# Writing out the order of three engines in the prologue of a two-layer graph network kernel

## The chip, the cores and the metric

The kernel runs on one core of a Trainium2 chip. The metric is the device time of one execution in microseconds (us). A core has five engines, each with its own instruction queue that runs in order: TensorE (PE, matrix products into PSUM), VectorE (DVE), ScalarE (ACT), GpSimd (POOL) and SyncE (SP, which here only issues DMAs). ScalarE and GpSimd issue DMAs from their queues too. An engine waits for another one through semaphores. "PEld" is the loading of weights into TensorE, a row of its own in the profile.

## The reference, cut to what matters

There are 6250 nodes with 128 features and 206250 edges, sorted by destination. Each edge has a type from 0 to 8.

```python
h = jnp.maximum(_layernorm(x), 0.0)
deg = segment_sum(ones, src);  norm = clip(deg, 1.0) ** -0.5
x = x + relu(segment_sum((h * norm)[src], dst)) @ W0.T + b0
h = jnp.maximum(_layernorm(x), 0.0)
msg = h[src] @ W_msg.T + b_msg + edge_embed[edge_type]
m = segment_sum(msg, dst)
x = x + gru_cell(m, h, W_ih, W_hh, b_ih, b_hh)
```

## The kernel before

The edge list is turned into a dense adjacency matrix of edge counts, 49 by 49 blocks of 128 by 128 (`NB` = 49), and each layer multiplies it from the left with a table of node features. The kernel has four stages.

**Prologue, edges** (lines 367 to 526). The lists `dst`, `src` and `etype` come in as tiles of 128 x 1616 integers (`dst_i`, `src_i`, `typ_i`), edge number j at partition j mod 128. Each is reduced to a small number per edge: `dst_f`, `low_b` (source mod 128), `code_b` (source div 128), `typ_b`. TensorE turns them by products with the identity (line 496), in four steps of `k0` with up to four column blocks each, and they are copied from PSUM to `turned` as 16-bit integers: fields 1 and 2 (code and type) by VectorE (line 506), fields 0 and 3 by ScalarE (line 508). SP writes them to a list in DRAM, `flat` (lines 516 and 521). Meanwhile a search finds where the edges of each window of 250 nodes begin: `heads` (every 128th destination) against `starts` gives `base_ps`, a product on TensorE (line 407); from it the addresses `base_i`, with which GpSimd fetches `span` (line 416); `search` compares it (line 446), `search_sums` adds up (line 454), and `last_of_search` turns the result into `row_i`, the row of `flat` at which each window starts (lines 468 to 484). The 49 blocks of x are loaded by SP in eight DMAs (lines 381 to 386); `stats` takes the layernorm statistics of a block (line 464).

**Prologue, windows** (lines 529 to 777). 25 windows are handled in seven groups of four (the last of one). `fetch` gathers the rows of `flat` from `row_i` (line 627, one indirect DMA per window on GpSimd), marks the edges that lie `inside` the window (641), masks the `fields` (648), turns them on TensorE (657), and ScalarE copies the types to `typ` and the code and low parts to `code_t` and `lo_t` (667, 670). `count` makes a mask per edge type, five on VectorE (`m_dve`, 682) and four on ScalarE (`m_act`, 685), sums them per node on TensorE (686) and copies the sums to `counts` (689). For each of seven chunks of seven blocks (`CB` = 7, `NCH` = 7), `degrees` sums the counts (696) and makes `scale` (704, square root on ScalarE 708), `rows_of` makes the reciprocal, `shift_`, and the scaled rows f (718 to 735), and `terms_of` splits them into the tables `tab1` (739 to 747): three bf16 terms in chunk 0 (`NARROW` = 1), two fp32r terms in the others. One pass of the loop at line 749 calls `degrees(i - 3)`, `fetch` of group i, `count` of group i - 1, then `rows_of` and `terms_of` of chunk i - 3. GpSimd also splits the small matrix `rest` in three (759, 761).

**First layer** (lines 803 to 931). The columns of the matrix are made in chunks (`FRONT`: one of 128 columns, then 24 of 256). `hots` makes a pair of one-hot tiles for 64 columns on VectorE (336), `build` multiplies them on TensorE (823) and ScalarE copies the counts to `adj` (832). While chunk c is built, the sums of chunk c - 1 run (`sums`, line 791): TOTAL = 105 products a chunk, spread over eight rounds. Those with `tab1[1]` and up need the matrix as fp32r (`cast`, 896, by ScalarE and VectorE in turn). SP writes `adj` to DRAM (929).

**Second layer** (lines 937 to 1085). It reads the matrix back, sums in the same way, and does the GRU.

What sets the order: inside `tc.manual_schedule(engines=...)` the instructions of the engines named keep the order of the program text. Before, VectorE alone is named in the prologue, and a scheduler places those of TensorE and ScalarE; in the first layer all three are named. A tile of a pool is reused when it is free; `reuse_waits="tile"` makes the wait for that one per tile.

Of the kernel before, what the change touches and what calls it, by code (L numbers as in the profile page):

```python
# [10 lines left out]
F32 = mybir.dt.float32  # L11
# [20 lines left out]
CB = 7  # L32
# [226 lines left out]
def by_matrix(  # L259
# [107 lines left out]
    with tc.tile_pool(name="pro", bufs=1) as pro, tc.manual_schedule(engines={mybir.EngineType.DVE}):  # L367
# [13 lines left out]
        for c in range(NCH):  # L381
            lo, hi = c * CB, min((c + 1) * CB, full)
            nc.sync.dma_start(
                out=xs[:, lo:hi, :], in_=x[lo * P : hi * P, :].rearrange("(b p) f -> p b f", p=P)
            )
        nc.sync.dma_start(out=xs[:tail, full, :], in_=x[full * P : N, :])
# [19 lines left out]
        for j in range(GT):  # L406
            nc.tensor.matmul(base_ps, less[:, j, :], one_b[:NG, :], start=(j == 0), stop=(j == GT - 1))
        base = pro.tile([P, 1], F32, name="base")
# [14 lines left out]


        dst_f = raw.tile([P, NT], F32, name="dst_f")
        nc.scalar.copy(dst_f, dst_i)
        low_i = raw.tile([P, NT], I32, name="low_i")
        nc.vector.tensor_scalar(low_i, src_i, P - 1, None, op0=ALU.bitwise_and)
        low_b = raw.tile([P, NT], BF16, name="low_b")
        nc.scalar.copy(low_b, low_i)  # L430
        nc.vector.tensor_scalar(src_i, src_i, 7, None, op0=ALU.logical_shift_right)
        code_b = raw.tile([P, NT], BF16, name="code_b")
        nc.vector.tensor_copy(code_b, src_i)
        typ_b = raw.tile([P, NT], BF16, name="typ_b")
        nc.vector.tensor_scalar(typ_b, typ_i, 0.0, float(TYPES - 1), op0=ALU.max, op1=ALU.min)
# [52 lines left out]
        for k0 in range(0, NT // P + 1, 4):  # L488
            k1 = min(k0 + 4, NT // P + 1)
            n = min(P, NT - k0 * P)  # L490
            for i, given in enumerate((dst_f, code_b, typ_b, low_b)):
# [17 lines left out]
            if k0 == 0:  # L509
                stats(8)  # L510
            if k0 == 4:
                search()
            if k0 == 8:
                search_sums()
# [22 lines left out]
        wnd = look.enter_context(tc.tile_pool(name="wnd", bufs=2))  # L537
        pps = look.enter_context(tc.tile_pool(name="turn_ps", bufs=5, space=PSUM))
        tps = look.enter_context(tc.tile_pool(name="sums_ps", bufs=2, space=PSUM))
        dps = look.enter_context(tc.tile_pool(name="deg_ps", bufs=1, space=PSUM))  # L540
# [38 lines left out]
        nc.gpsimd.memset(counts[:, WP * WB :, :], 0.0)  # L579

        stats(NB)
        mean = once.tile([P, NB], F32, name="mean")
        apart = pro.tile([P, NB], F32, name="apart")
        dev = once.tile([P, NB], F32, name="dev")
        nc.vector.tensor_sub(apart, st[:, :, 1], st[:, :, 4])
        nc.vector.tensor_add(dev, st[:, :, 2], st[:, :, 5])
        nc.vector.tensor_mul(apart, apart, apart)
        nc.vector.scalar_tensor_tensor(dev, apart, float(H // 4), dev, op0=ALU.mult, op1=ALU.add)
        nc.vector.tensor_scalar(dev, dev, 1.0 / H, EPS, op0=ALU.mult, op1=ALU.add)
        nc.vector.tensor_add(mean, st[:, :, 1], st[:, :, 4])  # L590

        nc.vector.tensor_add(brz, bih[:, :2], bhh[:, :2])
# [27 lines left out]
        groups = [(b, min(GB, WB - b)) for b in range(0, WB, GB)]  # L620
        typ_of = {}

        def fetch(b0_, nb):

            got = wnd.tile([P, GB, ROWS, 4, HALF], I16, name="got")
            for b in range(nb):
                nc.gpsimd.indirect_dma_start(  # L627
                    out=got[:, b].rearrange("p r f j -> p (r f j)"),
                    out_offset=None,
                    in_=edges_flat,  # L630
                    in_offset=bass.IndirectOffsetOnAxis(ap=row_i[:, b0_ + b : b0_ + b + 1], axis=0),
                )
            typ_of[b0_] = wnd.tile([P, GB * WP], BF16, name="typ")
            w0_ = b0_ * WP
            turns_ = {i: pps.tile([P, 4, P], F32, name="turn") for i in (1, 0, 2)}
            n = nb * ROWS
            g = got[:, :nb].rearrange("p b r f j -> p (b r) f j")
            inside = wnd.tile([P, 2, GB * ROWS, HALF], BF16, name="inside", bufs=1)
            fields = wnd.tile([P, GB * ROWS, 3, 2, HALF], BF16, name="fields")
            for d in range(2):  # L640
# [5 lines left out]
                )  # L646
            for d in range(2):
# [5 lines left out]
                )  # L653
            for i in (1, 0, 2):
                for b in range(nb):
                    for r in range(ROWS):
# [6 lines left out]
                        )  # L663
            for i in (1, 0, 2):
                ws = turns_[i][:, :nb, :WP]
# [8 lines left out]
        def count(b0_, nb):  # L674
# [4 lines left out]
            for k in range(TYPES):  # L679
                if k < first_level:  # L680
                    m = wnd.tile([P, GB * WP], BF16, name="m_dve", bufs=6)
                    nc.vector.tensor_scalar(m[:, :n], typ, float(1 + k), None, op0=ALU.is_equal)  # L682
                else:
                    m = wnd.tile([P, GB * WP], BF16, name="m_act", bufs=4)
                    nc.scalar.activation(m[:, :n], typ, AF.Sign, bias=levels[:, k - first_level : k - first_level + 1])
                nc.tensor.matmul(sums_t[:both, :n], sel[:, k, :], m[:, :n], start=(k == 0), stop=False)
# [62 lines left out]
        for i in range(NCH):  # L749
            if i >= 3:  # L750
                degrees(i - 3)
# [386 lines left out]
```

## Time and profile before

| | us |
|---|---|
| three timed runs | 948.75, 948.32, 945.35 (median 948.32) |
| the profiled execution | 949.22 |
| its span, first to last instruction | 947.1 |
| TensorE busy | 873.4 (92%) |
| VectorE busy | 816.0 (86%) |
| ScalarE busy | 733.8 (77%) |
| mean granted TensorE clock | 0.965 |

The span is counted from the first instruction. "Busy" leaves out waiting and the issuing of DMAs. A line of a timeline has the start, the busy time, the engine and line, and in brackets how long the engine sat idle before it and what ended that.

Some moments of the prologue before, in us from the start of the span:

| | us |
|---|---|
| `dst_f` starts on ScalarE | 8.57 |
| `row_i` is written | 30.67 |
| first window fetch on GpSimd | 31.25 |
| first `inside` on VectorE | 38.55 |
| last `inside` group starts | 87.15 |
| first one-hots start | 95.47 |
| first sums of the first layer | 112.6 |

### The profile page before, as it was taken

The numbers are of one execution on the slowest core, as the hardware profiler recorded it, in microseconds if no ns is written. First come the engines' busy times: TensorE is split into PE (matmuls) and PEld (weight loads), VectorE is DVE, ScalarE is ACT, GpSimd is POOL, SyncE is SP. The second block draws the span as 40 slices with busy tenths as digits, with TensorE's granted clock in tenths as the row PEclk, the third lists the DMA queues.
The fourth block names the chain that finished last, engine by engine and source line by source line (L and its number), as shares of the span: only waits on it lengthen the run. The fifth ranks groups of instructions, "written<-read, shape, count | busy, mean of one in ns | idle before, by whom it ended". The sixth has DMA issues, their size and how long they took to land.

```text
span 947.1 us, 25090 instructions
## 1 busy us (share of the span) xinstructions
PE 873.4 (92%) x11009; PEld 726.6 (77%) x11009; DVE 816.0 (86%) x908; ACT 733.8 (77%) x1397; POOL 40.6 (4%) x78
## 2 busy tenths in 40 slices
PE   3476599999999999999999988999999999999995
PEld 3354399899999989989999987776777777777775
DVE  5879988999999999999999949988988888877754
ACT  3287889999999999999999968766676676666753
POOL 3570000000000000000000000000000000000000
PEclk9579599999999999999999998999999999999998
DMA  9430345576476467557646786777777677666641
GB/s 279 134 118 9 71 134 155 170 205 176 145 205 200 140 186 205 159 162 204 185 138 203 205 288 200 260 252 262 276 242 256 221 272 273 218 239 236 227 117 32
DMA packets 201340, 181.34 MB, mean 191 GB/s; under 512 B 10695, under 2 KB 189627, under 8 KB 201067
## 3 DMA queue, kind: packets, MB, share of 16 engines
q1 hardware_dynamic: 198946, 173.41, 58.8%
q0 software_dynamic: 1664, 4.95, 1.7%
q8 instruction: 88, 1.44, 0.6%
q10 hardware_dynamic: 612, 1.30, 0.4%
q14 instruction: 30, 0.25, 0.1%
HBM read 95.75 MB, written 83.87 MB: 190 GB/s over the span
## 4 chain that ended last, share of the span: by engine, by line
PE 76%; DVE 11%; DMA 6%; ACT 3%; issue 3%; POOL 1%; SPq 0%; DVEq 0%; ACTq 0%
PE acc L791 54%; PE ev L823 10%; DMA piece<-adj_d 3%; DVE wide L1057 3%; PE gate L982 3%; PE gate L994 2%; DVE leave L1030 2%; PE acc L847 2%; DMA adj_d<-adj 1%; DVE fields L648 1%; PE turn L657 1%; ACT wide L1050 1%; DMA dst_i<-in_dst_dram 1%; PE tr L1015 1%; POOL got L627 1%
## 5 line engine op out<-in xcount | busy, mean ns | idle before, releaser
L791 PE MATMUL acc<-wide,tab 128*128 128x256 f32 (+2 forms) x3374 | 591.7, 327 | 4.9 <-DVE tab L956 3.7
L791 PEld LDWEIGHTS acc<-wide,tab 128*128 128x128 f32 x3374 | 492.3, 189 | 62.9 <-issue 10.6
L832 ACT CAST adj<-ev 128x784 bf16<-128x784 f32 x392 | 298.8, 819 | 31.4 <-PE ev L823 28.4
L1050 ACT ACTIVATE wide<-piece 128x512 fp32r<-128x512 bf16 (+1 forms) x336 | 200.8, 601 | 53.4 <-issue 37.6
L336 DVE TENSOR_TENSOR hot_l<-lo_t,iota 128x4096 bf16<-128x4096 bf16 x97 | 221.5, 2283 | 0.5 <-PE ev L823 0.5
L1030 DVE TENSOR_REDUCE leave<-piece 128x7 f32<-128x3584 bf16 (+2 forms) x43 | 154.8, 3601 | 16.4 <-DMA piece<-adj_d 16.3
L896 ACT CAST wide<-adj 128x1792 fp32r<-128x1792 bf16 (+1 forms) x75 | 125.0, 1667 | 3.7 <-PE acc L791 2.9
L823 PE MATMUL ev<-hot_c,hot_l 64*128 64x49 bf16 x6208 | 114.2, 183 | 7.4 <-DVE hot_c L336 4.1
L823 PEld LDWEIGHTS <-hot_l 64*128 64x128 bf16 x6208 | 93.0, 93 | 35.9 <-issue 8.9
L1057 DVE CAST wide<-piece 128x3584 fp32r<-128x3584 bf16 (+2 forms) x43 | 82.5, 1919 | 16.9 <-PE acc L791 16.9
L336 DVE TENSOR_TENSOR hot_c<-code_t,iota 128x1600 bf16<-128x1600 bf16 x97 | 95.4, 983 | 0.0
L896 DVE CAST wide<-adj 128x1792 fp32r<-128x1792 bf16 (+1 forms) x75 | 80.9, 1079 | 9.9 <-ACT adj L832 6.9
L791 PE MATMUL acc<-adj,tab 128*128 128x256 bf16 x525 | 67.2, 277 | 0.0
L1050 ACT ACTIVATION_READ_ACCUMULATOR wide<-piece 128x1 f32 x336 | 63.3, 188 | 0.0
L791 PEld LDWEIGHTS <-tab 128*128 128x128 bf16 x525 | 47.9, 99 | 7.5
L987 ACT COPY sum_sb<-acc 128x512 f32<-128x512 f32 (+2 forms) x13 | 7.3, 562 | 57.0 <-PE acc L791 57.0
L994 PE MATMUL gate<-sum_sb,wsum_sb 128*128 128x512 f32 (+2 forms) x78 | 35.0, 585 | 0.1
L982 PE MATMUL gate<-hT,whh_sb 128*128 128x512 f32 (+2 forms) x78 | 33.8, 569 | 0.0
L657 PE MATMUL turn<-ident_b,fields 128*128 128x128 bf16 x225 | 20.7, 276 | 12.6 <-DVE fields L648 12.6
L657 PEld LDWEIGHTS <-fields 128*128 128x128 bf16 x225 | 19.3, 129 | 14.8 <-DVE fields L648 14.8
L627 POOL DMA_INDIRECT got<-flat,row_i x25 | 26.4, 1055 | 13.3 <-DVE m_dve L682 6.8
L954 ACT ACTIVATE f<-xs,sh,rstd 128x128 f32<-128x128 f32 x49 | 19.5, 481 | 7.0 <-DMA adj_d<-adj 3.4
(163 smaller groups left out, 504.8 us busy)
## 6 DMA issues: line engine op xcount, KB each, us to landing
adj_d<-adj SPq DMA_DIRECT2D x24, 3136.0 KB
piece<-adj_d SPq DMA_DIRECT2D x77, 896.0 KB
piece<-adj_d SPq DMA_DIRECT2D x14, 672.0 KB
piece<-adj_d SPq DMA_DIRECT2D x7, 448.0 KB
out_dram<-res SPq DMA_DIRECT2D x11, 256.0 KB
xs<-in_x_dram SPq DMA_DIRECT2D x6, 448.0 KB
adj_d<-adj SPq DMA_DIRECT2D x1, 1568.0 KB
flat<-turned SPq DMA_DIRECT2D x3, 512.0 KB
```

What stands on the lines that cost most here:

```text
L336: nc.vector.tensor_tensor(to.rearrange("p j (k t) -> p j k t", t=2), twice.unsqueeze(2).to_broadcast([P, n, m // 2, 2]), of[:, :m].rearran ...
L627: nc.gpsimd.indirect_dma_start(out=got[:, b].rearrange("p r f j -> p (r f j)"), out_offset=None, in_=edges_flat, in_offset=bass.IndirectOf ...
L657: nc.tensor.matmul(turns_[i][:, b, :], fields[:, b * ROWS + r, i].rearrange("p d j -> p (d j)"), ident_b, start=(r == 0), stop=(r == ROWS ...
L791: nc.tensor.matmul(acc[:, : 2 * P].rearrange("f (t n) -> f t n", t=2) if twice else acc[:, :nd], tab[:, s, i, :], a[:, i, :P].unsqueeze(1) ...
L823: nc.tensor.matmul(ps[:, d, j * NB : (j + 1) * NB], hot_l[half, t, :], hot_c[half, t, :NB], start=True, stop=True,)
L832: nc.scalar.copy(adj[:, :, part * 16 : (part + 1) * 16].rearrange("p n (j d) -> p n j d", d=2), ps[:, :, : 8 * NB].rearrange("p d (j n) -> ...
L896: make(wide[q][:, :, :n], done[:, q * HP : (q + 1) * HP, :n])
L982: nc.tensor.matmul(ps[:, :nd], whh_sb[:, g * H : (g + 1) * H], hT[:, :nd], start=True, stop=(g == 2))
L994: nc.tensor.matmul(ps[:, :nd], wsum_sb[:, g * H : (g + 1) * H], sum_sb[:, :nd], start=False, stop=True)
L1030: nc.vector.tensor_reduce(leave[:, q * HP : (q + 1) * HP, c], piece, AX.X, ALU.add)
L1050: nc.scalar.activation(pieces[q][:, i, :nd], piece[:, i, :nd], AF.Copy, accum_out=leave[:, q * HP + i, c : c + 1],)
L1057: nc.vector.tensor_copy(pieces[q][:, :, :nd], piece[:, :, :nd])
```

## The change

TensorE and ScalarE are added to `manual_schedule` in the prologue, so that all three engines keep the order of the text, and the text is reordered.

- The x loads go from SP to ScalarE's queue, behind `dst_f`, as three DMAs of 16 blocks and one of the rest. The product `base_ps` is ahead of the turns on TensorE. The turns of a step run in the order dst, low, type, code.
- `search` and `search_sums` come one step of `k0` sooner; the statistics that stood there are taken later: 11 and 20 ahead of the first group, the last 18 and what is made from them behind it (`rest_of_stats`).
- The groups are of 3, 4, 4, 4, 4, 4 and 2 windows. `fetch` of group i + 1 is issued ahead of the work on group i.
- `inside_of` and `count` are generators, run in steps, so that counts of group i - 2, masks of group i - 1 and windows of group i are interleaved; degrees of a chunk are asked for two passes after its last group. `shifts` is taken out of `rows_of`.
- Of the rows f, ScalarE makes three of seven in chunks 0 to 3, five in chunk 4, and all in chunks 5 and 6 (before: none in chunks 0 to 3, all in 4 to 6).
- The memset of the end of `counts` goes from GpSimd to VectorE.
- In the first layer, chunk 1 begins with 35 of its 105 sums (`lead`) ahead of its first build; the others are spread over the seven later rounds.

```diff
-    with tc.tile_pool(name="pro", bufs=1) as pro, tc.manual_schedule(engines={mybir.EngineType.DVE}):
+    with tc.tile_pool(name="pro", bufs=1) as pro, tc.manual_schedule(
+        engines={mybir.EngineType.PE, mybir.EngineType.Activation, mybir.EngineType.DVE}
+    ):
...
-        for c in range(NCH):
-            lo, hi = c * CB, min((c + 1) * CB, full)
-            nc.sync.dma_start(
-                out=xs[:, lo:hi, :], in_=x[lo * P : hi * P, :].rearrange("(b p) f -> p b f", p=P)
-            )
-        nc.sync.dma_start(out=xs[:tail, full, :], in_=x[full * P : N, :])
...
+        dst_f = raw.tile([P, NT], F32, name="dst_f")
+        nc.scalar.copy(dst_f, dst_i)
+        for lo in range(0, full, 16):
+            nc.scalar.dma_start(
+                out=xs[:, lo : lo + 16, :],
+                in_=x[lo * P : (lo + 16) * P, :].rearrange("(b p) f -> p b f", p=P),
+            )
+        nc.scalar.dma_start(out=xs[:tail, full, :], in_=x[full * P : N, :])
+        low_i = raw.tile([P, NT], I32, name="low_i")
+        nc.vector.tensor_scalar(low_i, src_i, P - 1, None, op0=ALU.bitwise_and)
...
-            for i, given in enumerate((dst_f, code_b, typ_b, low_b)):
+            for i, given in ((0, dst_f), (3, low_b), (2, typ_b), (1, code_b)):
...
             if k0 == 0:
-                stats(8)
+                search()
             if k0 == 4:
-                search()
-            if k0 == 8:
                 search_sums()
...
-        groups = [(b, min(GB, WB - b)) for b in range(0, WB, GB)]
+        at = [0, *range(3, WB, GB), WB]
+        groups = [(b, to - b) for b, to in zip(at, at[1:])]
...
-        for i in range(NCH):
-            if i >= 3:
-                degrees(i - 3)
-            fetch(*groups[i])
-            if i >= 1:
-                count(*groups[i - 1])
-            if i >= 3:
-                rows_of(i - 3)
-                terms_of(i - 3)
+        ends = list(itertools.accumulate(n for _, n in groups))
+        last = [min(g for g, n in enumerate(ends) if 2 * WP * n >= min((c + 1) * CB * P, N)) for c in range(NCH)]
+        deg_at = {i: [c for c in range(NCH) if last[c] + 2 == i] for i in range(NCH + 2)}
+        rows_at = {4: (0, 3), 5: (1, 3), 6: (2, 3)}
+        olds = {g: count(*groups[g]) for g in range(NCH)}
+        fetch(*groups[0])
+        for i in range(NCH):
+            if i + 1 < NCH:
+                fetch(*groups[i + 1])
+            new = inside_of(*groups[i])
+            old, older = olds.get(i - 1, iter(())), olds.get(i - 2, iter(()))
+            run(older, 1)
+            run(old, 1)
+            run(new, 1)
+            degrees(deg_at[i])
+            run(new, 1)
+            for c in deg_at[i]:
+                scales(c)
+                root(c)
+            run(old, 1)
+            if i == 0:
+                rest_of_stats()
+            if i in rows_at:
+                c, n = rows_at[i]
+                rows_of(c, range(n, CB), range(n))
+            run(new, 2)
+            run(old, 1)
+            if i in rows_at:
+                terms_of(c)
+            for c in deg_at[i]:
+                shifts(c)
...
-        degrees(NCH - 3)
-        count(*groups[NCH - 1])
-        rows_of(NCH - 3)
-        degrees(NCH - 2)
+
+        run(olds[NCH - 2], 1)
+        run(olds[NCH - 1], 1)
+        degrees([NCH - 2])
+        run(olds[NCH - 1], 1)
+        scales(NCH - 2)
+        root(NCH - 2)
+        rows_of(NCH - 4, range(3, CB), range(3))
+        run(olds[NCH - 1], 1)
         early_hots = [hots(0)]
-        rows_of(NCH - 2)
-        degrees(NCH - 1)
+        run(olds[NCH - 1], 1)
+        terms_of(NCH - 4)
+        shifts(NCH - 2)
+        rows_of(NCH - 3, range(5, CB), range(5))
+        rows_of(NCH - 2, (), range(CB))
+        degrees([NCH - 1])
...
-            ends = spread(TOTAL, rounds)
+            lead = (NARROW * SPL + 2) * HP if c == 1 else 0
+            ends = spread(TOTAL - lead, rounds) if c != 1 else [0, *spread(TOTAL - lead, rounds - 1)]
...
+                if r == 0:
+                    run(steps, lead)
```

## The prediction

> **What bounds the kernel now.** I read the busy slices first, then the busy time by stretches of 10 us, then the chain that ended last, then each engine's timeline up to 118 us.
>
> The slices (each digit is the busy share of 23.7 us in tenths; PEclk the granted clock):
>
> ```profile
> PE   3476599999999999999999988999999999999995
> DVE  5879988999999999999999949988988888877754
> ACT  3287889999999999999999968766676676666753
> PEclk9579599999999999999999998999999999999998
> ```
>
> TensorE is full from the sixth slice on, and not before. By stretches (busy us of each engine, clock, DMA share, GB/s):
>
> ```profile
> 100.00:110.00 10.00, 3.20 (x110) 2.46 (x104) 9.70 (x11) 9.97 (x22) 0.00 (x0) 0.50 0.01 2
> ...
> 120.00:130.00 10.00, 10.00 (x216) 9.21 (x216) 8.10 (x6) 7.80 (x11) 0.00 (x0) 1.00 0.01 3
> ```
>
> From 120 to 180 us TensorE has 10.00 of every 10 us, so in the first layer it sets the end, and the change reaches the end only through the moment at which its stream gets going. The chain gives this moment (start, us, what):
>
> ```profile
> 108.59 2.17 issue
> 110.77 0.99 DVE hot_c L336
> 111.81 0.85 PE ev L823 x32
> 112.66 2.89 PE acc L791 x13
> ...
> 118.35 1.74 PE acc L791 x13
> ```
>
> TensorE waits for the third pair of one-hots, which VectorE ends at 111.75; chunk 1 starts at 111.81 and chunk 2 at 131.52. Before it, VectorE is the bound: between its first `inside` (38.55) and 111.75 the six idle stretches of its timeline are 1.84+1.88+2.90+0.72+0.21+0.51 = 8.1 us, so 65.1 us of work. And the windows could not be fetched before 31.25:
>
> ```profile
> 31.25 0.95 POOL L627 DMA_INDIRECT got<-flat,row_i  x1 [0.57 <-DVE row_i L484]
> ```
>
> I reckon in two pieces: up to this first `got` (G = 31.25), and from it to chunk 2 (131.52, G+100.3).
>
> **Piece 1: up to the first fetch.** The x loads go from SP to ScalarE's queue, between `dst_f` and `low_b`. Both queues before (start, us):
>
> ```profile
> 5.50 10.94 SPq L383 DMA_DIRECT2D xs<-in_x_dram  x7
> 16.55 1.25 SPq L386 DMA_DIRECT2D xs<-in_x_dram  x1
> 17.90 1.47 SPq L525 DMA_DIRECT2D flat<-far  x1
> ```
>
> ```profile
> 8.57 1.54 ACT L426 CAST dst_f<-dst_i 128x1616 f32<-128x1616 int32 x1 [3.98 <-DMA dst_i<-in_dst_dram]
> ...
> 14.47 1.54 ACT L430 CAST low_b<-low_i 128x1616 bf16<-128x1616 int32 x1 [1.54 <-DVE low_i L428]
> ```
>
> An issue takes 0.38 us where nothing is in front (the first two), but 1.51 each once loads stand ahead: at the 290 GB/s of 10 to 18 us, 0.459 MB takes 1.58. The x bytes start to move at about 9.1; when the fifth issue returns at 13.33, 1.23 of the 1.84 MB issued before it have moved, and at 16.44 2.13 of 2.75: an issue returns when all but 0.6 MB ahead of it has moved. ScalarE runs in order: its table load at 3.31 starts when its last issue ends, at 3.28. So: `dst_i` lands 0.2 sooner, since the weight loads (0.27 MB on ScalarE's queue) no longer share with it (8.35); `dst_f` to 9.9; bytes about 0.95 later (as from `src_i`'s issue at 0.75 to its first bytes, about 1.7), 10.85. The last issue has 3.15 MB ahead: (3.15-0.6)/0.29 = 8.8, so `low_b` starts near 19.6 instead of 14.47. The bounds: 11.7 if four issues cost 0.45 each, and 23.7 if ScalarE is held till the last of 3.2 MB has landed (11.0 to move, 1.8 to land, as `dst_i`'s bytes ended near 6.8 and it was read at 8.57). I take 19.6, since eight rows in SP's queue say so.
>
> The Trainium skill ("DMA: Bandwidth & Descriptors", Issuing engines are not separate DMA queues) says that the time to initiate a DMA on a sequencer "is usually small relative to the DMA itself". The SP rows disagree once loads queue up; by the rule the sum would be that of the first rival below.
>
> Queued behind on ScalarE are `low_b` and all `turned` copies; on TensorE the turns of `low_b` now stand ahead of those of `typ_b` and `code_b`, and VectorE waits for these. From `low_b` (21.15): the turns of typ and code end at about 21.7 and 22.2; VectorE copies them (0.65 each) to 23.1, `is_less` 1.8, two copies 1.3, the reduction and its two scalings 2.15, two copies 1.3, two small ones 0.45: 30.05; `row_t` 0.25, TensorE's ten matmuls 2.3, `row_i`: 32.8 (30.67 before). The earlier base (its sum is no longer behind the turns of `dst_f`; span fetch near 10.2 instead of 13.57) is worth nothing then: `is_less` stands at 23.1, after the span landed. The third flat write goes out at 29.65 (25.12 before), the small last one at 30.1. Its 0.52 MB need 0.9 to start and 1.5 at 0.35 MB/us (21 to 22 us of the trace), the last 0.2, the landing 1.9: 34.2. So G' = 34.3, 3.05 later; at the bounds 27.7 (the span gates then) and 38.4. The bias loads, now ahead of the flat writes on SP, run while SP waits anyway; the weight loads, now behind the copies on ScalarE (four issues, 2.04), land near 31 and are read after 32.6: no cost.
>
> **Piece 2: from the first fetch to chunk 2,** in us after G or G'.
>
> VectorE's work: 65.1, less ten row scalings that go to ScalarE (28 become 18, 1.91/7 = 0.27 each: 2.7), plus 18 statistics (0.196) and seven small steps (1.2) that stood before the first `inside`, under the fetch, and now stand behind it: 67.1. A first group of three windows lands after 2 x 1.25 + 3.55 = 6.05 (7.3 before).
>
> Its idle time, by a walk through the order written out, with back-to-back times: inside 0.95, fields 2.54, masks 0.99, scalings 1.09, terms 1.67 (3.46 for the first), shift 0.43; on ScalarE 0.47+0.89+0.89 (windows), 2.44 (masks), 1.29 (counts), 0.39 a row. The old waits for counts (2.90) go, as counts are now asked for two stages later. New: all five of GpSimd's casts and subtractions of `rest` stand between the fetches of groups 2 and 3 (1.9+1.9+0.9 = 4.7). Group 2's fetch starts when fields 0 is done (8.75) and its issues end at 13.5; casts to 18.3, issues to 22.05, landing 25.6; VectorE is there at 22.15: 3.45 idle. Sqrt behind a table load (1.28): 0.95. Terms that wait for ScalarE's rows: 1.05 in chunk 0, 0.4 in chunk 2. The last chunk's rows are on ScalarE, behind five `adj` copies: 1.65. Counts of group 5: 0.55. Sum 8.05; as back-to-back times leave some 1.5 of small gaps out, in which ScalarE catches up, I take 6.5 (5 to 9). Third one-hots done: 6.05+67.1+6.5 = 79.7 (80.5 before).
>
> The 35 leading sums need no one-hots, only chunk 0's last three copies, 0.72 each, after ScalarE's rows: 2.2 where VectorE needs 4.9 (terms, one-hots), so they start at 77.1. At the half clock of the 2.89 row: 13 x 0.222, then 22 x 0.135 = 5.9. Then 8 builds x 0.52 and 70 sums x 0.135 = 13.6: 96.6. Without the lead the same 105 sums follow 79.7. VectorE needs after 79.7 four pairs (3.17) and three casts (1.08), with 1.0 of waits for a free buffer: 96.6 as well. So G'+96.6 instead of G+100.3, a gain of 3.7 (1.5 to 5): VectorE and TensorE arrive together, and neither would let the other come sooner.
>
> **The sum.** 3.05 lost, 3.7 gained: 0.65 faster. Against the profiled execution: span 947.1 to 946.45, and with the 2.1 around it 949.2 to 948.55; the median of the three runs, 948.3, is 0.9 below its time, so I forecast 947.7, in round numbers 948; by the bounds of the gain and 1 us on either side in G', 945 to 951.
>
> **Rivals.**
> ScalarE is not held. For it: the 0.38 us issues, and loads of 1.05 MB in three issues instead of seven. Against: the 1.51 rows. `low_b` starts at 11.7, the span then gates `is_less` (near 16.5), 6.6 sooner than forecast; G' = 27.7, 3.55 sooner than before; with the gain 7.2 faster: 941.
>
> ScalarE is held until x has landed (slower). Place: the last x issue. `low_b` at 23.7, 4.1 later than forecast, nothing hides it: 3.45 slower, 951.8. It decides from 20.25 on, where loss and gain are equal. Against: SP's last x issue returned at 17.80, with about 0.7 MB to go.
>
> The lead buys nothing: VectorE and ScalarE (9.70 and 9.97 of 10 us in the stretch shown) pace chunk 1 and keep 19.7 from the third one-hots on. 79.7 against 80.5 gains 0.8, less 3.05: 2.2 slower, 950.5. Against: VectorE has 8.10 of 10 us from 120 to 130.
>
> **How the numbers follow.** Forecast 0.5, not held 0.24, held to the landing 0.1, no lead 0.16. The predicted time is the forecast's, 948. About 0.5% (4.7 us) is what a measurement can tell from no change here. Faster by more: nearly all of the first rival and 0.03 of the forecast, 0.26. Slower by more: where the two slow rivals meet or the stages stall more than my walk shows, 0.16. The rest, 0.58. The range 940 to 952.5 holds the first and the two slow rivals; 945 to 951 is the forecast's own.
>
> **What would show it.** Right: `low_b` near 19.6 with x issues of several us in ScalarE's queue; first `got` near 34; a wait of VectorE for `got` in the fourth group; sums of chunk 1 ahead of its first build, at about 111.4; chunk 2 near 131.2. Wrong: `low_b` before 14 (then 941), chunk 1's builds waiting for one-hots in every second round (950.5), or TensorE idle after 135, since then its stream is not what I shifted.

## The result and the profile after

| | before | after |
|---|---|---|
| median of five runs, us | 948.32 (944.52 to 948.75) | 955.64 (953.97 to 956.88) |
| span of the profiled execution, us | 947.1 | 954.8 |
| `low_b` starts | 14.47 | 18.52 |
| first fetch G | 31.25 | 33.91 |
| first `inside` | 38.55 | 39.53 |
| last `inside` group starts | 87.15 | 88.37 |
| third one-hots done | 111.75 | 119.70 |
| chunk 2 starts | 131.52 (G+100.3) | 139.96 (G+106.1) |

The change makes the kernel slower: ratio 1.0089, 95% interval 1.0063 to 1.0115. The forecast was 948.0. Chunk 2 starts 8.4 us later and the span is 7.7 us longer, so the place was right: what is lost is lost before chunk 2, and nearly all of it stays. Three of the five sets of experiments ran on other chips, where the kernel before takes 950 to 951 us; the kernel after, run again on two of these, takes 966. Kernels are therefore compared by their ratio to the kernel before in the same set.

The slices of after (busy share in tenths, 23.9 us each; PEclk the granted clock):

```profile
PE   2476499999999999999999997999999999999995
DVE  4877888999999999999999958988988888877754
ACT  2278879999999999999999968775676666766763
PEclk9678599999999999999999998999999999999998
```

The fifth slice of TensorE has 4 where it had 5: the full stream begins later, and is much the same from there on. By stretches (busy us of PE, PEld, DVE, ACT, POOL with the number of instructions; clock, DMA share, GB/s):

```profile
100.00:110.00 10.00, 4.38 (x83) 3.00 (x84) 9.90 (x16) 8.79 (x23) 0.00 (x0) 0.50 0.11 36
...
120.00:130.00 10.00, 7.92 (x173) 7.05 (x171) 8.37 (x7) 5.91 (x8) 0.00 (x0) 1.00 0.59 123
```

Before, TensorE had 10.00 us in the second of these, now 7.92, with ScalarE down from 7.80 to 5.91: no engine is full. The way to the first fetch went as reckoned. ScalarE's queue (start, us; what ended the idle time in brackets), and GpSimd's first fetch:

```profile
11.83 2.70 ACTq L408 DMA_DIRECT2D xs<-in_x_dram  x1
14.63 3.85 ACTq L412 DMA_DIRECT2D xs<-in_x_dram  x1
18.52 1.54 ACT L431 CAST low_b<-low_i 128x1616 bf16<-128x1616 int32 x1 [6.72 <-issue]
```

```profile
33.91 0.94 POOL L634 DMA_INDIRECT got<-flat,row_i  x1 [20.30 <-DMA flat<-turned]
```

ScalarE is held in the issues of the last two x loads, `low_b` starts late, and the landing of `flat` gates the fetch, as forecast. What went wrong lies behind it, in VectorE's waits (the five longest):

```profile
61.39 1.03 DVE L647 TENSOR_TENSOR inside<-got,mine 128x768 bf16<-128x768 int16 x2 [3.18 <-DMA got<-flat,row_i]
...
67.90 0.20 DVE L744 RECIPROCAL scale<-scale 128x7 f32<-128x7 f32 x1 [1.62 <-ACT scale L740]
...
73.06 0.17 DVE L733 SCALAR_TENSOR_TENSOR scale<-deg,dev 128x7 f32<-128x7 f32 x1 [1.18 <-PE deg L721]
...
92.80 0.17 DVE L733 SCALAR_TENSOR_TENSOR scale<-deg,dev 128x7 f32<-128x7 f32 x1 [2.47 <-PE deg L721]
...
114.72 0.63 DVE L773 TENSOR_SCALAR tab<-f 128x896 fp32r<-128x896 f32 x1 [1.94 <-ACT f L767]
```

With three shorter ones (0.80, 1.02, 0.25) they make 12.5 us between 39.53 and 119.70; before, 8.1. Where the 2.47 us come from is read on TensorE and ScalarE around 90 us:

```profile
84.18 4.02 PE L666 MATMUL turn<-ident_b,fields 128*128 128x128 bf16 x36 [3.76 <-DVE fields L656]
88.13 1.44 PE L705 MATMUL sums<-m_act,sel 128*59 128x500 bf16 x4
89.41 1.22 PE L705 MATMUL sums<-m_dve,sel 128*59 128x500 bf16 x5
...
92.46 0.30 PE L721 MATMUL deg<-ones_b,counts 9*128 9x1 bf16 x6 [1.41 <-ACT counts L709]
```

```profile
90.98 1.42 ACT L709 CAST counts<-sums 27x500 bf16<-27x500 f32 x2 [1.76 <-PE sums L706]
```

TensorE turns the sixth group (4.02 us here, at a granted clock of 0.50; the 36 turns at 57.14, at a clock of 1.00, take 2.18) ahead of the sums of the fifth, ScalarE's counts wait for the sums, `deg` waits for the counts, and `scale`, next in VectorE's order, waits for `deg`. But the turns stood ahead of these sums before, too. TensorE and VectorE before, at the same place:

```profile
82.13 3.69 PE L657 MATMUL turn<-ident_b,fields 128*128 128x128 bf16 x36 [2.01 <-DVE fields L648]
85.75 1.24 PE L686 MATMUL sums<-m_dve,sel 128*59 128x500 bf16 x5
...
89.98 0.25 PE L696 MATMUL deg<-ones_b,counts 9*128 9x1 bf16 x4 [1.67 <-ACT scale L708]
```

```profile
81.99 1.07 DVE L682 TENSOR_SCALAR m_dve<-typ 128x500 bf16<-128x500 bf16 x5
...
94.05 0.16 DVE L704 SCALAR_TENSOR_TENSOR scale<-deg,dev 128x7 f32<-128x7 f32 x1
```

VectorE after, its work for the fifth group's masks and the last work ahead of the wait:

```profile
84.18 1.07 DVE L701 TENSOR_SCALAR m_dve<-typ 128x500 bf16<-128x500 bf16 x5
...
88.91 1.42 DVE L656 TENSOR_TENSOR fields<-got,inside 128x1152 bf16<-128x1152 int16 x2
```

From the end of the fifth group's masks on VectorE to the end of `deg` it takes 7.2 us before (83.06 to 90.23) and 7.5 after (85.25 to 92.76): the chain is about as long. What changed is when VectorE comes for it: 11.0 us behind the masks before, 5.1 after (90.33). Before, a chunk's degrees were asked for at the start of the third pass after its last group; after, in the middle of the second. They are asked for sooner, not later.

The chain that ended last, from the window before chunk 1's builds (start, us, what):

```profile
112.03 2.66 ACT f L767 x7
114.69 2.13 ACT adj L904 x3
...
116.87 5.50 PE acc L863 x35
...
122.71 2.96 ACT adj L904 x4
125.68 1.53 ACT adj L904 x2
127.21 0.85 ACT wide L970
```

The 35 leading sums run from 116.87 to 122.36. The third one-hots are done at 119.70 and wait for them, and ScalarE, with no build to copy, idles 4.93 us; afterwards its copies set the pace.

### The profile page after: what moved, and what is told of

Same layout as the page of the kernel before. It is cut to its first block, busy times and chain, and to the rows that moved or that the text cites. A ratio compares the mean times of both kernels' runs of the same rounds, so it can differ in the third digit from the quotient of the medians.

```text
span 954.8 us, 25081 instructions
## 1 busy us (share of the span) xinstructions
PE 874.8 (92%) x11009; PEld 727.6 (76%) x11009; DVE 813.8 (85%) x899; ACT 737.2 (77%) x1410; POOL 39.9 (4%) x77
## 4 chain that ended last, share of the span: by engine, by line
PE 75%; DVE 8%; DMA 6%; ACT 5%; issue 3%; POOL 2%; ACTq 1%; SPq 0%; DVEq 0%; POOLq 0%
PE acc L863 54%; PE ev L895 10%; DMA piece<-adj_d 3%; PE gate L1058 3%; PE gate L1070 2%; DVE wide L1133 2%; PE acc L919 2%; DMA adj_d<-adj 1%; DVE leave L1106 1%; POOL got L634 1%; ACT adj L904 1%; ACT wide L1126 1%; PE turn L666 1%; PE tr L1091 1%; DMA bih<-in_L_b_ih_dram 1%
## 5 line engine op out<-in xcount | busy, mean ns | idle before, releaser
L895 PE MATMUL ev<-hot_c,hot_l 64*128 64x49 bf16 x6208 | 114.1, 182 | 5.2 <-ACT adj L904 2.8
L666 PEld LDWEIGHTS <-fields 128*128 128x128 bf16 x225 | 19.0, 126 | 19.2 <-DVE fields L656 11.1
L634 POOL DMA_INDIRECT got<-flat,row_i x25 | 25.5, 1020 | 29.5 <-DMA flat<-turned 20.3
```

The costliest lines, as they stand in the source:

```text
L634: nc.gpsimd.indirect_dma_start(out=got_of[b0_][:, b].rearrange("p r f j -> p (r f j)"), out_offset=None, in_=edges_flat, in_offset=bass.In ...
L666: nc.tensor.matmul(turns_[i][:, b, :], fields[:, b * ROWS + r, i].rearrange("p d j -> p (d j)"), ident_b, start=(r == 0), stop=(r == ROWS ...
L895: nc.tensor.matmul(ps[:, d, j * NB : (j + 1) * NB], hot_l[half, t, :], hot_c[half, t, :NB], start=True, stop=True,)
```

## The experiments

G is the first fetch; "one-hots" and "chunk 2" are, as moments after G, the cast on VectorE that follows the third one-hots, and the first cast of chunk 2, from one profile each. The last column is the ratio of the timed runs to the kernel before in the same set, with its interval.

| kernel | G | one-hots | chunk 2 | ratio |
|---|---|---|---|---|
| before | 31.25 | +80.4 | +99.8 | 1 |
| after | 33.91 | +85.7 | +106.1 | 1.0089 (1.0063 to 1.0115) |
| no lead | 34.69 | +85.5 | +104.5 | 1.0094 (1.0079 to 1.0109) |
| x on SP | 31.83 | +86.6 | +106.9 | 1.0081 (1.0068 to 1.0095) |
| GpSimd in hand order | 35.24 | +87.7 | +108.0 | 1.0140 (1.0120 to 1.0161) |
| scales late | 34.41 | +86.2 | +106.5 | 1.0117 (1.0100 to 1.0135) |
| old pass, first try | 38.25 | +80.4 | +99.5 | 1.0083 (1.0066 to 1.0100) |
| old edge part | 32.07 | +82.7 | +103.0 | 1.0045 (1.0029 to 1.0061) |
| rows sooner | 35.03 | +90.3 | +111.1 | 1.0175 (1.0154 to 1.0196) |
| VectorE alone in hand order | 35.40 | +85.5 | +105.0 | 1.0100 (1.0083 to 1.0117) |
| *other chips:* | | | | |
| after (in two sets) | 35.56, 34.50 | +94.0, +93.8 | +114.4, +114.1 | 1.0158 (1.0117 to 1.0198), 1.0161 (1.0142 to 1.0180) |
| statistics first (in two sets) | 36.54, 34.26 | +93.6, +92.7 | +113.9, +113.0 | 1.0163 (1.0142 to 1.0184), 1.0159 (1.0126 to 1.0191) |
| rows back (in two sets) | 33.76, 34.01 | +93.2, +93.5 | +115.9, +114.6 | 1.0168 (1.0141 to 1.0195), 1.0171 (1.0141 to 1.0202) |
| old pass, statistics kept | 36.59 | +88.8 | +108.3 | 1.0102 (1.0081 to 1.0123) |
| sooner fetch, old pass | 28.34 | +93.6 | +112.9 | 1.0049 (1.0031 to 1.0067) |
| the same, terms on VectorE (in two sets) | 28.41, 28.48 | +86.1, +85.9 | +105.4, +104.9 | 1.0024 (1.0001 to 1.0046), 0.9993 (0.9976 to 1.0011) |

### One part undone each: lead, x loads, GpSimd's casts, scales

```diff
-            lead = (NARROW * SPL + 2) * HP if c == 1 else 0
-            ends = spread(TOTAL - lead, rounds) if c != 1 else [0, *spread(TOTAL - lead, rounds - 1)]
+            lead = 0
+            ends = spread(TOTAL, rounds)
```

> The changed kernel with its 35 leading sums of chunk 1 put back among the eight rounds. My theory now: the lead costs time, since ScalarE has nothing to copy while it runs (idle 4.93 us from 117.8 to 122.7 in the profile of after) and then paces chunk 1. Without it the first build of chunk 1 should come when the third one-hots are done (119.7) instead of at 122.3, and chunk 2 some 1 to 2.5 us sooner than at 139.9: 1 to 2.5 us faster than after. Rival, the reasoning of my forecast: the lead saves TensorE work behind the one-hots, and without it chunk 2 comes 2 to 4 us later.

No difference: 955.71. Without the lead TensorE stands still until the one-hots are there,

```profile
120.33 0.85 PE L895 MATMUL ev<-hot_c,hot_l 64*128 64x49 bf16 x32 [7.21 <-DVE hot_c L336]
```

but chunk 1 starts at 120.33 instead of 122.36, and ScalarE has its copies sooner. From the one-hots to chunk 2 it takes 19.1 us, and 20.3 with the lead. The work brought forward comes back as a later start of the builds.

For the second, the x loads went back to SP, ahead of everything else that it issues:

```diff
-            nc.scalar.dma_start(
-                out=xs[:, lo : lo + 16, :],
...
+            nc.sync.dma_start(
+                out=xs[:, lo:hi, :], in_=x[lo * P : hi * P, :].rearrange("(b p) f -> p b f", p=P)
```

> The changed kernel with the x loads back on SP as before, and nothing else. Theory: ScalarE's queue, held by the x issues until 18.5, delays the first window fetch; with low_b near 9.6 the search waits for the span alone (lands near 16.5), and the first fetch comes near 28 instead of 33.9: about 6 us faster than after. Rival: the fetch is late because of the new order of turns and of the flat writes, whatever queue has x: fetch near 33 still, less than 1 us gained.

954.67. `low_b` starts at 9.11, and `row_i` is there at 27.62, but the first fetch only at 31.83: SP, held by x until 16.9, sends the first `flat` write at 17.03 and the last at 26.67. So 2.1 of the 5.9 us expected there are won, and half of that is lost again as VectorE waits longer for `deg` (4.42 us in all) and the square root (2.15).

For the third, `mybir.EngineType.Pool` was added to the engines of `manual_schedule`, so that GpSimd's five casts and subtractions of `rest` stand behind all 25 fetches, as in the text:

> The changed kernel with GpSimd's order written out as well, so that the five casts and subtractions of rest come behind all 25 window fetches. Theory: they hold the fetch of group 3 (VectorE idle 3.18 us at 61.4 in after) and slow the masks that run beside them (five masks 2.56 us instead of about 1); without them the fourth group starts near 56.5 and the kernel is 3 to 5 us faster than after. Rival: what is gained there is waited for again at the counts and the square roots: under 1 us.

958.55, slower. VectorE waits 4.37 us for the fourth group all the same: its first fetch alone took 5.05 us on GpSimd, where the others of this kernel take 0.9 to 1.6. Why is not known.

For the fourth, VectorE's `scale` and `root` were moved behind the masks and rows of the pass:

```diff
-            for c in deg_at[i]:
-                scales(c)
-                root(c)
             run(old, 1)
...
             if i in rows_at:
                 c, n = rows_at[i]
                 rows_of(c, range(n, CB), range(n))
+            for d in deg_at[i]:
+                scales(d)
+                root(d)
             run(new, 2)
```

> The changed kernel with scales and root of a pass moved behind the masks and rows of that pass. Theory: VectorE waits in order for degrees whose counts are not yet copied (1.18, 2.47 and 0.25 us in after), because the sums of a group stand behind the turns of the next one on TensorE; with the scales later these waits go, 2 to 3.5 us faster than after. Rival: ScalarE paces these passes, and the wait comes back in front of the rows or the shifts: under 1 us.

958.03, no gain; the intervals (1.0100 to 1.0135, and 1.0063 to 1.0115 for after) overlap, so that slower is not shown either. The waits for `deg` shrink from 3.90 to 1.98 us when they are asked for later, and come back as waits for the square root (2.24) and for ScalarE's rows (1.53 and 2.93). None of these four parts, undone alone, gives the loss back, and with the x loads and the scales what was won came up again as other waits.

### The two halves apart

The edge part of one kernel was put ahead of the window pass and first layer of the other, with the hand order of each (here the old pass; the other way round the engines change places):

```diff
+        order.enter_context(tc.manual_schedule(engines={mybir.EngineType.PE, mybir.EngineType.Activation, mybir.EngineType.DVE}))
...
         look.close()
+        order.close()
+        order.enter_context(tc.manual_schedule(engines={mybir.EngineType.DVE}))
```

In the third of these runs the second context begins behind the statistics and `brz`.

> The edge part of the kernel before (x loads on SP) with the window pass (three engines in hand order, lag of a stage, groups of 3 and 4) and the first layer of the kernel after. Theory that the parts add up and the pass itself is the larger loss: first fetch near 31.3, third one-hots near 31.3 + 85.8 = 117, first cast of chunk 2 near 137, time about 953, ratio 1.005 to 1.006. Rival, the pass is harmless and the late start is the cause: third one-hots at 112 to 113, time 946 to 949.

> The edge part of the kernel after (x loads on ScalarE, base first, search one step sooner, three engines in hand order) with the window pass and the first layer of the kernel before (VectorE alone in hand order, groups of four, no lag, no lead). Theory: the two parts add up. The edge part costs the 2.7 us by which the first fetch is late, and the pass and all behind it run as before: first fetch near 33.9, third one-hots near 33.9 + 80.5 = 114.4, first cast of chunk 2 near 134, time about 951, ratio 1.003. Rival: the late start, with statistics and weight products still to be made behind it, spoils the old pass too: third one-hots at 117 or later, time 953 to 956.

> The edge part of the kernel after with the window pass and first layer of the kernel before, as in the first run of this kind, but with all statistics kept behind row_i, which had stood ahead of the copies there and made the first fetch 4.3 us later than in the kernel after. Theory that edge part and pass add up: first fetch near 33.9, third one-hots at about 114.4, chunk 2 at 133.5 to 134.2, ratio 1.002 to 1.004, some 5 us less than the kernel after beside it. Rival, the old pass can't keep its length behind this edge part: within 2 us of the kernel after.

The new pass behind the old edge part takes 951.51, ratio 1.0045: half the loss. Its longer waits on VectorE are nearly those of after:

```profile
57.42 1.03 DVE L651 TENSOR_TENSOR inside<-got,mine 128x768 bf16<-128x768 int16 x2 [3.01 <-DMA got<-flat,row_i]
...
64.81 0.20 DVE L748 RECIPROCAL scale<-scale 128x7 f32<-128x7 f32 x1 [2.25 <-ACT scale L744]
...
87.89 0.17 DVE L737 SCALAR_TENSOR_TENSOR scale<-deg,dev 128x7 f32<-128x7 f32 x1 [1.70 <-PE deg L725]
...
109.84 0.63 DVE L777 TENSOR_SCALAR tab<-f 128x896 fp32r<-128x896 f32 x1 [1.94 <-ACT f L771]
```

The first try of the reverse was spoiled: 29 statistics had moved ahead of the copies that feed `flat`, where they waited for x, and G came at 38.25. It still shows that the old pass keeps its length from the first fetch to within 0.3 us (+80.4, +99.5) even when it starts 7 us later: the lateness goes through in full, and the old pass has no trouble with it. With the statistics kept behind `row_i`, on another chip, the old pass takes 960.38 where the kernel after takes 966.39 in the same set: 6.0 us for the pass (in the two profiles chunk 2 comes 3.8 us sooner). The first fetch was at 36.59 there, and VectorE waits 8.23 us for `deg` once, so the ratio of 1.0102 isn't that of the edge part alone.

### Which part of the pass

```diff
-        rows_at = {4: (0, 3), 5: (1, 3), 6: (2, 3)}
+        rows_at = {5: (2, 3), 6: (3, 3)}
+        ends_at = {3: (0, 3), 4: (1, 3)}
...
             for c in deg_at[i]:
                 shifts(c)
+            if i in ends_at:
+                c, n = ends_at[i]
+                rows_of(c, range(n, CB), range(n))
+                terms_of(c)
```

> The kernel after, with the lag of rows and tables undone: rows f and tables of chunks 0 and 1 at the end of passes 3 and 4, those of chunks 2 and 3 in passes 5 and 6, none left for the tail but chunks 4 to 6. Theory: the lag puts one chunk's work on VectorE (3.2 us) behind the last window while VectorE idles in the passes before; sooner rows fill that idle time, third one-hots near 116.5 instead of 119.7, time 952 to 953. Rival: the loop from the turns over ScalarE's copies, sums and counts to the degrees sets the pace, so that rows that come sooner wait for the square root and for ScalarE instead: third one-hots at 119 to 121, time 955 to 956.

962.76, much slower, the opposite of the theory. VectorE's waits in this kernel:

```profile
68.81 0.20 DVE L744 RECIPROCAL scale<-scale 128x7 f32<-128x7 f32 x1 [1.84 <-ACT scale L740]
...
72.34 0.63 DVE L773 TENSOR_SCALAR tab<-f 128x896 bf16<-128x896 f32 x1 [1.98 <-ACT f L767]
...
85.55 0.63 DVE L773 TENSOR_SCALAR tab<-f 128x896 fp32r<-128x896 f32 x1 [3.13 <-ACT f L767]
```

Rows and tables that come sooner wait for the square root and for ScalarE's rows, and hold `inside` of the next group meanwhile. Given the new interleaving, the lag is of use. The rival names the waits that came, but not their size: it had 955 to 956. That the loop over TensorE and ScalarE sets the pace, and not VectorE's place for the rows, fits this run and is not shown by it alone.

The next kernel has the `manual_schedule(engines={mybir.EngineType.DVE})` of before in the prologue, and is else that of after.

> The kernel after, with VectorE alone in hand order in the prologue (TensorE and ScalarE placed by the scheduler again, the text as in after). Theory: TensorE's order written out, in which sums of the masks and degrees stand behind the turns of the next group, makes VectorE's waits for deg (1.18 + 2.47 + 0.25 us); without it they go: third one-hots near 116, time about 952. Rival: the order of VectorE's own text makes them, as the scheduler can't ask for degrees sooner than VectorE makes the masks: third one-hots at 119 to 120, time 954 to 956.

956.98: with the scheduler's order of TensorE and ScalarE the waits for `deg` stay (0.51, 2.10, 2.20, 1.66 us, in sum more than the 3.90 of after), while those for the square root go; all waits together are 12.3 us against 12.5. So naming the two engines doesn't make them. What is left is the order of the text, in which VectorE asks for the degrees a pass sooner.

The last two edits were undone by themselves:

```diff
+        rest_of_stats()
         fetch(*groups[0])
...
-            if i == 0:
-                rest_of_stats()
```

```diff
-        rows_at = {4: (0, 3), 5: (1, 3), 6: (2, 3)}
+        rows_at = {4: (0, 0), 5: (1, 0), 6: (2, 0)}
...
-        rows_of(NCH - 4, range(3, CB), range(3))
+        rows_of(NCH - 4, range(CB), ())
...
-        rows_of(NCH - 3, range(5, CB), range(5))
+        rows_of(NCH - 3, (), range(CB))
```

> The kernel after, with the last 18 statistics and the seven small steps moved back ahead of the first window (VectorE idles 3.9 us there). Theory: nothing is won, since the second group's windows land near 46.1 (last fetch issued at 41.5 for 1.6 us, about 3 us to land) and the fourth group is waited for anyway (3.18 us): the 4.8 us turn into waits for got, third one-hots at 118.5 to 120, time 954.5 to 956. Rival: VectorE's work is what counts, third one-hots near 116, time 952.

> The kernel after, with the rows f of chunks 0 to 3 back on VectorE (12 rows, 3.3 us more for it) and all of chunk 4 on ScalarE (2 rows less), so ScalarE has 10 rows of 0.4 us less. Theory that the loop over ScalarE (turns, copies, sums, counts, degrees, square root, rows) sets the pace: VectorE's added work falls into its waits, third one-hots at 118.5 to 120.5, time 954 to 956. Rival, VectorE's work sets it: 2.7 us later, third one-hots near 122.4, time 958.

Both came out near 966.5, which neither theory had. ScalarE stood still in them for several microseconds at a time. So the kernel after was run as a control beside them, and both again:

> The kernel after, unchanged, as a control for the runs beside it. In the last three kernels VectorE, ScalarE and TensorE stood still for 3 to 8 us at a time between 52 and 73 us, in waits that no engine of the core ends. Theory that such waits belong to the chip on which they ran: they can show here too, then the time is above ratio 1.009, and the other kernels of this call are read against this one. Theory that they belong to those kernels: none here, ratio 1.008 to 1.010, third one-hots at 119 to 121.

> The kernel with the last statistics ahead of the first window once more. If the long waits belonged to the chip: 954.5 to 956.5, ratio 1.008 to 1.010, third one-hots at 118.5 to 120 (the statistics' 4.8 us come back as waits for got and deg). If VectorE's work counts: third one-hots near 116, ratio 1.005. If the long waits belong to this kernel: above ratio 1.015 again.

> The kernel with the rows f of chunks 0 to 3 back on VectorE once more. If the long waits belonged to the chip: ratio 1.008 to 1.011, VectorE's 2.7 us more of work fall into its waits for ScalarE and deg. If VectorE's work counts: third one-hots 2.7 us later, near 122.4, ratio 1.012. If the long waits belong to this kernel: above 1.015 again.

> The kernel after, unchanged, as a control for the runs beside it: ratio 1.009 on a chip without the long waits, 1.016 on one with them.

The control itself takes 965.73, so the long waits come with the chip and not with the two edits. ScalarE in the control:

```profile
65.79 0.99 ACT L684 CAST code_t<-turn 128x1000 bf16<-128x1000 f32 x1 [2.59 <-PE sums L706]
70.07 0.99 ACT L684 CAST lo_t<-turn 128x1000 bf16<-128x1000 f32 x1 [3.29 <-remote]
72.93 1.43 ACT L709 CAST counts<-sums 27x500 bf16<-27x500 f32 x2 [1.87 <-remote]
```

Beside it, statistics first (964.91) and rows back (966.22) make no difference that can be measured. The 3.3 us of row scalings given to ScalarE and the 4.8 us of statistics put behind the first window are both paid for in waits either way, on this chip at least.

### A sooner first fetch with the old pass

The old pass behind the new edge part with the x loads on SP, the search later, and, from the second of these runs on, the casts of `rest` on VectorE ahead of the first window:

```diff
-            if k0 == 0:
+            if k0 == 8:
                 search()
-            if k0 == 4:
+            if k0 == 12:
                 search_sums()
...
-            nc.gpsimd.tensor_copy(terms[:, s, :], rest)
+            nc.vector.tensor_copy(terms[:, s, :], rest)
             if s + 1 < SPL:
-                nc.gpsimd.tensor_sub(rest, rest, terms[:, s, :])
+                nc.vector.tensor_sub(rest, rest, terms[:, s, :])
```

> The window pass and first layer of the kernel before (VectorE alone in hand order), behind an edge part made from the kernel after: base_ps and dst_f first, three engines in hand order, but the x loads on SP and the search two steps of k0 later, so that VectorE doesn't wait for span ahead of the copies that feed the flat writes. Theory: the old pass keeps its length from the first fetch (third one-hots at +80.5, chunk 2 at +99.5 to +100.3), so what the first fetch gains is gained in full: row_i near 25, first fetch at 26 to 27, chunk 2 near 126, time 942 to 944, ratio 0.995, faster than both. Rival: SP, held by x until 17, sends the flat writes too late, first fetch at 29 to 31, time 946 to 948.

> The old window pass behind the sooner first fetch, and the five casts and differences of rest on VectorE ahead of the first window, so that GpSimd fetches without a break (they stood for 4.4 us between its second and third group, and VectorE then waited 4.33 us for got). Theory: first fetch near 28, third group there at 48 to 49, third one-hots at 106 to 108, chunk 2 at 126 to 127, ratio 0.993 to 0.997, faster than both kernels. Rival: the five operations and the casts' place cost VectorE what GpSimd gains, ratio 0.998 to 1.002. With long waits as in the last call: above 1.003.

> The old pass behind the sooner first fetch with the casts of rest on VectorE, once more. Where the control shows no long waits: 1.9 us for lo_t and 4.0 us for the sums' masks go, and of the 7.0 us wait for deg some 5: third one-hots near 108, ratio 0.994 to 0.998, faster than both kernels. If the ratio stays above 1.001 the wait for deg is made by the order in which ScalarE's masks were placed, not by the chip.

The edge part did what was meant: first fetch at 28.4, 2.8 us sooner than before. The gain isn't kept. The first of the three (955.33) waits 4.33 us for the third group, behind GpSimd's casts of `rest`, and 7.81 for `deg`. With the casts on VectorE the kernel is equal to the one before (0.9993, 0.9976 to 1.0011) or a little slower (1.0024). In the last run VectorE's fourth group waits at

```profile
62.80 0.17 DVE L706 SCALAR_TENSOR_TENSOR scale<-deg,dev 128x7 f32<-128x7 f32 x1 [7.48 <-PE deg L698]
```

for sums whose masks ScalarE made late. In both of these runs TensorE turns the first two groups in one stretch and ScalarE's last masks of the first group stand behind the copies of the second, as the scheduler placed them; the long waits of these chips (1.89 and 3.36 us ahead of `lo_t`) come on top. How much each has of the 7.5 us stays open, and no version was found that beats the kernel before.

## Why the prediction was wrong

**Piece 1 was right.** `low_b` at 19.6: measured 18.52, and 19.6 as the mean of the fourteen profiles with the x loads on ScalarE (18.31 to 21.10). The four issues took 0.83, 0.71, 2.70 and 3.85 us, so "ScalarE is not held" fell, and "held until x has landed" (23.7) as well. First fetch 34.3: measured 33.91, and 34.8 as the mean of twelve profiles with this edge part. The Trainium skill's rule that issuing a DMA "is usually small relative to the DMA itself" (page "DMA: Bandwidth & Descriptors", Issuing engines are not separate DMA queues) does not hold here, where loads stand ahead in the queue: the last issue held ScalarE 3.85 us.

**The work of Piece 2 was right**: 67.1 forecast, 67.7 measured (80.2 less 12.5).

**Its idle time failed**: 6.5 forecast with bounds of 5 to 9, 12.5 measured. By the walk's own terms: waiting for the fourth group 3.45, measured 3.18; square root 0.95, 1.62; terms waiting for ScalarE's rows 1.05 + 0.4 + 1.65, measured 0.80 + 1.02 + 1.94; counts of group 5 0.55, but the waits for `deg` are 1.18 + 2.47 + 0.25 = 3.90. That is the term mis-sized most, by 3.35: the step "the old waits for counts (2.90) go, as counts are now asked for two stages later" misread the order. Degrees had been asked for in the third pass after a group and are now asked for in the second; for the fifth group VectorE comes 5.1 us behind its masks instead of 11.0, and turns, sums, counts and `deg` need 7.5. The second fault is the step from 8.05 to 6.5: the small gaps "in which ScalarE catches up" took nothing off the waits. ScalarE is part of the loop. Third one-hots: G'+79.7 forecast, G'+85.8 measured.

**The lead failed too**: started at G'+77.1 in the forecast, G'+83.0 measured; 5.5 us long where 5.9 was reckoned; then 17.6 to chunk 2 instead of 13.6. "VectorE and TensorE arrive together, and neither would let the other come sooner" left out ScalarE, which had nothing to copy while the leading sums ran and was the pacer after them. The rival "the lead buys nothing" had the mechanism (19.7 from the one-hots on; 20.3 measured), and the run without the lead, which takes the same time, agrees.

**The sum**: 3.05 lost and 3.7 gained, forecast 0.65 faster. Measured in the one profile: 2.66 lost at the first fetch and 5.8 behind it (G+106.1 against G+100.3). The two halves run apart give some 4 us for the pass (951.51 against 947.44) and the other half, by the difference, for the edge part. The edge part's half is read as the later fetch and the eight statistics fewer that are made ahead of the first window: between the first and the second `inside` it is 7.42 us in after and 5.97 with the old edge part. For the pass the profile with the old edge part shows 11.1 us of waits instead of 8.1 and 20.3 us instead of 19.4 from the one-hots to chunk 2. What is shown is that no single edit of the pass that was tried, undone, gives it back; that degrees asked for sooner than the loop over TensorE's turns and ScalarE's counts can give them are its cause is read from the waits, from the run with late scales and from that with sooner rows. No run shortens the loop or puts the degrees back by a whole pass, so this stays open.

## What to carry to other kernels

When a wait is to go because its result is asked for later, measure in the old and in the new order how far the asking stands behind the work that feeds it, and how long the chain between them takes through every engine's queue: here 11.0 us had become 5.1, and the chain from masks over sums and counts to `deg` took 7.5. An idle sum from a walk with back-to-back times was too low here (8.05 against 12.5), where three engines feed each other in a ring; take nothing off it. Work brought forward on the busiest engine is worth something only if the engines that feed the rest can go on meanwhile; and a control belongs beside every comparison, on the same chip.

## What the runs showed of the hardware

VectorE's and GpSimd's elementwise work hold each other up. VectorE's five masks of 128 x 375 in after, and GpSimd's two subtractions beside them; the first begins while VectorE makes `fields`, until 50.81:

```profile
50.73 2.56 DVE L701 TENSOR_SCALAR m_dve<-typ 128x375 bf16<-128x375 bf16 x5
```

```profile
49.68 1.85 POOL L820 TENSOR_TENSOR adj<-adj 9x384 f32<-9x384 f32 x1
...
52.25 0.92 POOL L820 TENSOR_TENSOR adj<-adj 9x384 f32<-9x384 f32 x1
```

In the kernel with GpSimd's casts behind the fetches the same five masks take 0.92 us, and the subtraction takes 0.85 in the kernel before at 42.56, where VectorE is idle. Of the 2.56 us the first mask (50.73) and the last (52.37) have 0.92 each, beside the first and the second subtraction. Fetches hardly have this effect: at 57.00, beside them, five masks of 500 columns take 1.20, and 1.07 at 84.18, where GpSimd does nothing.

The kernel after takes 955.6 us on one chip and 966 on two others, and the kernel before 947 to 948 on the first and 950 to 951 on the others. In the kernels profiled on the others, between 44 and 73 us, while the windows are fetched, ScalarE, and in some kernels TensorE and VectorE, wait up to 4.8 us at a time, and the profile puts it down to "remote", to nothing on this core. What it is was not found; during the three waits of the control that are so marked (2.84, 3.29 and 1.87 us) no block of instructions is moved by DMA. Each of these chips was used at one time only, so that the chip and the time are not told apart. A change in this stretch can therefore cost 0.9% in one place and 1.6% in another.
